# Layer 0 of a two-layer graph-attention kernel: per-node sums in sixteen 32x32 tiles of TensorE in place of four 64x64 tiles

## The chip, the cores and the metric

The kernel runs on one core of a Trainium2 chip. The metric is device time in microseconds (us), from the start to the end of one execution; lower is better. The core has five engines with a queue of instructions each: TensorE (PE; its weight loads are shown apart as PEld), VectorE (DVE), ScalarE (ACT), GpSimd (POOL) and SyncE (SP). Sixteen DMA engines move data between the chip's memory and the on-chip memory (128 partitions). [...]

## The reference

Eight graphs share one adjacency of 2048 nodes, and each node has 256 float32 features. Two attention layers are applied, each with a residual and a layer norm over the features:

```python
# layer 0
e = leaky_relu(einsum('bnd,bmd->bnm', x @ W1, x @ W2), 0.2)
e = where(adj > 0, e, -1e12)
x = layernorm(x + relu(einsum('bnm,bmd->bnd', softmax(e), x @ W3)))
# layer 1: 4 heads of 64; q = x @ W
e = leaky_relu(e_src[:, :, None, :] + e_dst[:, None, :, :], 0.2)
e = where(adj > 0, e, -9e15)
x = layernorm(x + elu(einsum('bijh,bjhd->bihd', softmax(e, axis=2), q)))
```

The adjacency is sparse (each entry is set with a chance of 1/256, then made symmetric, and each node is its own neighbour), so a node has about 17 neighbours, and only their rows are needed.

## The kernel before

**Nodes, tiles, units.** Nodes are ranked by their number of neighbours and cut into 16 tiles of 128 nodes. Tile `t` has `SLOTS[t]` slots (36, 23, 22, 20, 20, 19, 18, 17, 17, 16, 16, 15, 14, 14, 13, 11): slot `k` of a tile is the k-th neighbour of each of its 128 nodes. The eight graphs are worked in two halves `h` of `HB` = 4 graphs. A *unit* is one tile, one half and one layer; there are 32 units for each layer. In layer 0 units with 16 slots or more are cut in two *parts* (22 of the 32 units), the others have one. Tile 0 has 26 main slots and one extra row that serves its ten rare further slots, so a half has 281 main slots, and layer 0 has 562.

**A slot of layer 0.** POOL issues an indirect DMA (`gather`, L203) that brings 128 rows of 4 x 256 float32 (512 KB) into half of a ring tile. There are 16 ring tiles of two slots (`RING`, `CHUNK`) and three more that are held for other use. DVE makes the four dot products of each row with the node's own projected row (`dots`, L726). After the last slot of a part come the softmax steps (`logits0`, `weights0`). ACT then writes, for each slot and each of the four graphs `b`, a 128x64 matrix `dg` with the node's weight on two stacked 64x64 diagonals (`weighted`, L936: `twice` scaled by one column of weights). PE adds weight times row into the accumulators as a matmul of that diagonal with the gathered rows (`add_slot`, L900): eight matmuls of a 64x64 tile, each over 256 columns, for two halves `r` of the nodes, two pairs `c` of graphs, and two graphs `j` in a pair. Each float32 matmul shows as two records in the trace, so a slot has 16. The four (r, c) tiles of the array are independent. The sum of a part lies in two accumulators, `acc[r]`, with partition 64c + node-of-half and column j*256 + feature; `psa` has four banks, so the two of the next part are free while one part is being read. When PE is done with a ring tile, the tile is free for a later gather (`credits`).

**Joining and finishing.** At slot 4 of a second part ACT copies the accumulators of the first part into `hs` (L1023), scaled by the share `u.fs` that the first part keeps in the joint softmax (`spread_shares`, L875); DVE adds the second part's (L1037). In a unit of one part ACT copies (L1041). PE transposes `hs` (`turn`, L501), multiplies by W3 (`project`, L509), DVE applies relu and adds the residual `u.xr` (`residual`, L1054), and the layer norm, the store to `x1s`, the projection for layer 1 (`queries`, L1095), its own terms (`own_terms`, L1111) and the scatter to the table `qg` (`store`, L211) follow. All of these carry the order (half, pair): partition 64c + p holds node p of half r in columns r*512. So `before0` first gathers the node's own rows in node order into one buffer `xo` (`own_rows`), and four SP DMAs (L703) rearrange it into `u.xr`; the x1 rows in `x1s` are kept in that order too, and layer 1 reads them back with one DMA (L1290). The scatter to `qg` goes in two DMAs with half rows.

**The order of work.** Python generators write the instructions of DVE, ACT and PE in a fixed order, the calendar: `tick` runs once for each slot that PE sums; in it `due(n, ...)` events fall n ticks later, ACT draws diagonals two slots ahead (`AHEAD`), and DVE runs up to the next part's slots plus 9 ahead (`SLACK`). Each engine works strictly in its written order and waits on semaphores.

**Layer 1** (L1290 and later) gathers rows of `qg`, DVE or ACT scales them by the weights, and PE sums them with `ident` in four 64x64 tiles. It shares `add_slot` with layer 0.

Of the kernel before, what the change touches and what calls it, by code (L numbers as in the profile page):

```python
# [27 lines left out]
H = 4  # L28
# [111 lines left out]
def fast_path(  # L140
# [43 lines left out]
    dp = ctx.enter_context(tc.tile_pool(name="diag", bufs=4))  # L184
# [46 lines left out]
    q_rows = held[2][:, 2 * KC * C :][:, : 2 * (QW + 2 * H)].rearrange("p (r w) -> p r w", r=2)  # L231
# [8 lines left out]
    twice = const.tile([P, 64], F32, tag="twice", name="twice")  # L240
    nc.vector.tensor_tensor(twice, ident[:, :64], ident[:, 64:], ALU.add)
# [33 lines left out]
    spare = q_rows.rearrange("p r w -> p (r w)")  # L275
# [255 lines left out]
    class Unit:  # L531
        def __init__(self, layer, h, t):
# [22 lines left out]
            self.xo = None  # L555
            self.ready = self.turned = False
# [135 lines left out]
    def own_rows(u):  # L692
        u.xo = xo_rows
        gather(u.xo, xg[u.h][:, :], order[:, u.t : u.t + 1])

    def before0(u):
        while u.xo is None:
            yield
        xo = u.xo
        u.xr = xrp.tile([P, 2, HW], F32, tag="xr", name=f"xr_{u.name}")  # L700
        for r in range(2):
            for c in range(2):
                nc.sync.dma_start(  # L703
                    u.xr[64 * c : 64 * c + 64, r, :], xo[64 * r : 64 * r + 64, ts(c, HW)]
                )
# [3 lines left out]
        turn(xo, f"x_{u.name}", xT)  # L709
        u.turned = True  # L710
# [120 lines left out]
    def weights0(u, i, K, e, m):  # L831
# [7 lines left out]
        if i == len(u.parts) - 1:  # L839
# [5 lines left out]
            if i:  # L845
                due(2, spread_shares, u, e[:, :, 0])
# [19 lines left out]

    def spread_shares(u, f):

        G = 2 if u.layer == 0 else HG // 2
        fs = sp.tile([P, 2, G], F32, tag=f"f{u.layer}", name=f"f_{u.name}", bufs=2 - u.layer)  # L870
# [15 lines left out]
    def add_slot(acc, k, K, rows, diag):  # L886

        for j in range(1 if diag is None else 2):  # L890
            for c in range(2):
                for r in range(2):
                    rr = slice(64 * r, 64 * r + 64)
                    if diag is None:
                        out, lhsT = acc[r][64 * c : 64 * c + 64, :], ident[rr, rr]
                        rhs = rows[rr, ts(c, 2 * CD)].rearrange("p (j w) -> p j w", j=2)[:, :, :C]
                    else:
                        out, lhsT = acc[r][64 * c : 64 * c + 64, ts(j, C)], diag[rr, 2 * c + j, :]
                        rhs = rows[rr, ts(2 * c + j, C)]
# [130 lines left out]
    def after0(u):  # L1030
# [57 lines left out]
        def queries(r):  # L1088
            if r == 0:
                u.qrow = q_rows  # L1090
# [694 lines left out]
```

## Time and profile before

| what | value |
|---|---|
| median of 12 runs | 2449.03 us (2440.92 to 2455.49) |
| the profiled execution's own time | 2447.55 us |
| span of its profile | 2445.6 us |
| matmuls of layer 0's sums (L900, `acc<-s,dg`) | 8992 records, 152.9 to 1422.0 us of the span |
| matmuls of layer 1's sums (L900, `acc<-s,ident`) | 4496 records, 1424.2 to 2426.2 us |
| diagonals (L936) | 2248 of 128x64, mean 340 ns |
| dot products (L726) | 2248 of 128x256, mean 419 ns |
| first part's copies to `hs` (L1023) | 88 of 128x256, mean 463 ns |
| second part's additions on DVE (L1037) | 44 of 128x512, mean 680 ns |
| rearranging DMAs `xr<-held` (L703) | 128 of 128 KB |
| DMA in all | 734.64 MB, mean 300 GB/s |

The 2445.6 us thus fall into a setup of some 153 us, 1270 us of layer 0, and 1020 us of layer 1. The engines run at the same time, so the busy times are not a sum. Durations in a row are those of one instruction from start to end; instructions of one engine overlap at their ends, so the pitch of a series (first start to last end, divided by its number) is smaller than the mean duration.

### The profile page before, as it was taken

The numbers are of one execution on the slowest core, as the hardware profiler recorded it, in microseconds if no ns is written. First come the engines' busy times: TensorE is split into PE (matmuls) and PEld (weight loads), VectorE is DVE, ScalarE is ACT, GpSimd is POOL, SyncE is SP. The second block draws the span as 40 slices with busy tenths as digits, with TensorE's granted clock in tenths as the row PEclk, the third lists the DMA queues.
The fourth block names the chain that finished last, engine by engine and source line by source line (L and its number), as shares of the span: only waits on it lengthen the run. The fifth ranks groups of instructions, "written<-read, shape, count | busy, mean of one in ns | idle before, by whom it ended". The sixth has DMA issues, their size and how long they took to land. (4 is left out here: it accounts for less than half of the span.)

```text
span 2445.6 us, 50606 instructions
## 1 busy us (share of the span) xinstructions
PE 2039.0 (83%) x16234; PEld 1086.2 (44%) x16234; DVE 1950.1 (80%) x6799; ACT 1405.2 (57%) x4803; POOL 1438.0 (59%) x1411
## 2 busy tenths in 40 slices
PE   5158999889889999999999988888788788888885
PEld 2135565556555566656666532222233222332331
DVE  7398788888978886888788568788877787887877
ACT  6035676566666677777677565443554646443545
POOL 3254555555655656555555566667666666766662
PEclk9578898999999999999999998888888887888888
DMA  9987999888887889898888799988998998989981
GB/s 379 340 286 260 303 312 321 264 310 276 294 288 239 292 297 305 302 303 284 304 280 299 261 339 333 322 312 313 331 338 310 316 347 306 337 307 331 329 305 42
DMA packets 239648, 734.64 MB, mean 300 GB/s; under 512 B 53456, under 2 KB 62800, under 8 KB 236944
## 3 DMA queue, kind: packets, MB, share of 16 engines
q0 software_dynamic: 182784, 645.78, 75.6%
q1 hardware_dynamic: 55360, 84.44, 10.2%
q8 instruction: 132, 2.16, 0.3%
q14 instruction: 140, 1.15, 0.1%
q10 hardware_dynamic: 1232, 1.11, 0.1%
HBM read 674.46 MB, written 76.02 MB: 307 GB/s over the span
## 5 line engine op out<-in xcount | busy, mean ns | idle before, releaser
L900 PE MATMUL acc<-s,ident 64*64 64x512 f32 x4496 | 808.6, 681 | 166.3 <-issue 134.4
L203 POOL DMA_INDIRECT s<-xg,idx x564 | 593.5, 1052 | 498.9 <-PE acc L900 268.1
L726 DVE CUSTOM_DVE_ANT_0 j<-s,held 128x256 bf16<-128x256 f32 x2248 | 798.6, 419 | 65.3 <-DMA s<-xg,idx 51.4
L900 PE MATMUL acc<-s,dg 64*64 64x256 f32 x8992 | 707.5, 399 | 103.5 <-issue 56.7
L203 POOL DMA_INDIRECT s<-qg,idx x564 | 569.0, 1009 | 293.3 <-issue 144.7
L936 ACT ACTIVATE dg<-twice,e 128x64 f32<-128x64 f32 x2248 | 574.6, 340 | 88.3 <-remote 46.5
L900 PEld LDWEIGHTS acc<-s,ident 64*64 64x64 f32 x4496 | 284.6, 150 | 678.3 <-issue 608.9
L900 PEld LDWEIGHTS acc<-s,dg 64*64 64x64 f32 x8992 | 390.5, 137 | 374.7 <-issue 199.8
L983 DVE TENSOR_TENSOR s<-s,p 128x2048 f32<-128x2048 f32 (+1 forms) x246 | 542.3, 2208 | 0.1
L973 ACT ACTIVATE s<-s,e 128x64 f32<-128x64 f32 x1376 | 343.5, 335 | 73.1 <-DVE e L1238 32.2
L726 DVE DVE_READ_ACCUMULATOR2_ANT e<- 128x1 f32 x2248 | 180.8, 80 | 0.5 <-DMA s<-xg,idx 0.3
L211 POOL DMA_INDIRECT out_dram<-o,oidx x128 | 128.6, 1005 | 72.2 <-ACT o L487 34.8
L1434 ACT ACTIVATE e<-e 128x40 f32<-128x40 f32 (+19 forms) x88 | 27.4, 312 | 219.8 <-issue 93.2
L1095 PE MATMUL ps_q<-wqs,x1T 128*128 128x264 f32 x512 | 134.1, 402 | 6.7 <-issue 2.9
L509 PE MATMUL ps_p_g<-held,xT 128*128 128x256 f32 x512 | 126.4, 400 | 15.6 <-ACT xT L1434 14.0
L509 PE MATMUL ps_p_h<-held,hT 128*128 128x256 f32 x512 | 121.8, 390 | 0.1
L509 PEld LDWEIGHTS ps_p_g<-held,xT 128*128 128x128 f32 x512 | 99.3, 199 | 42.1 <-ACT xT L1434 14.6
L1095 PEld LDWEIGHTS ps_q<-wqs,x1T 128*128 128x128 f32 x512 | 93.7, 192 | 46.6 <-issue 22.9
L1434 ACT COPY held<-ps_q 128x264 f32<-128x264 f32 x128 | 46.4, 379 | 115.3 <-PE ps_q L1095 87.3
L509 PEld LDWEIGHTS ps_p_h<-held,hT 128*128 128x128 f32 x512 | 95.9, 193 | 27.0 <-issue 13.6
L1054 DVE SCALAR_TENSOR_TENSOR y<-ps_p_h,xr 128x512 f32<-128x512 f32 x64 | 44.0, 687 | 79.0 <-PE ps_p_h L509 52.9
L1162 DVE TENSOR_TENSOR e<-s,own 128x32 f32<-128x32 f32 (+1 forms) x290 | 52.3, 184 | 63.3 <-DMA s<-qg,idx 57.0
(206 smaller groups left out, 1554.4 us busy)
## 6 DMA issues: line engine op xcount, KB each, us to landing
adj<-in_adj_dram SPq DMA_DIRECT2D x16, 1024.0 KB
xr<-held SPq DMA_DIRECT2D x128, 128.0 KB
x1s<-y SPq DMA_DIRECT2D x32, 512.0 KB
xr<-x1s SPq DMA_DIRECT2D x32, 512.0 KB
s<-xg,idx POOLq DMA_INDIRECT x564
s<-qg,idx POOLq DMA_INDIRECT x564
edges<-adj SPq DMA_DIRECT2D x16, 512.0 KB
xg<-in_x_dram SPq DMA_DIRECT2D x4, 2048.0 KB
```

The costliest lines, as they stand in the source:

```text
L203: nc.gpsimd.indirect_dma_start(out=dst, out_offset=None, in_=table, in_offset=AT(ap=index, axis=0), bounds_check=table.shape[0] - 1, oob_i ...
L211: ins = nc.gpsimd.indirect_dma_start(out=table, out_offset=AT(ap=index, axis=0), in_=src, in_offset=None)
L509: nc.tensor.matmul(pp[:, ts(j, C)], lhsT=srcT[:, ts((2 * i + j) * KC + k, P)], rhs=weight[:, k, :], start=(k == 0), stop=(k == KC - 1),)
L726: nc.vector.tensor_tensor_reduce(out=jt, in0=rows[:, ts(b, C)], in1=others(b), scale=1.0, scalar=0.0, op0=ALU.mult, op1=ALU.add, accum_out ...
L900: nc.tensor.matmul(out, lhsT=lhsT, rhs=rhs, start=(k == 0 and j == 0), stop=(k == K - 1 and (j == 1 or diag is None)), tile_position=(64 * ...
L936: nc.scalar.activation(diag[:, b, :], twice, AF.Copy, scale=u.p[i][:, b, k : k + 1])
L973: nc.scalar.activation(v[:, a, g, :], v[:, a, g, :], AF.Copy, scale=pv[:, a, g : g + 1])
L983: nc.vector.tensor_tensor(v, v, pv.unsqueeze(3).to_broadcast([P, n, H, D]), ALU.mult)
L1054: nc.vector.scalar_tensor_tensor(u.y[:, ts(i, 512)], pp, 0.0, u.xr[:, i, :], ALU.max, ALU.add)
L1095: nc.tensor.matmul(pq[:, : C + 2 * H], lhsT=u.x1T[:, ts(i * KC + k, P)], rhs=w.sqs[:, k, j * H : j * H + CD + H], start=(k == 0), stop=(k ...
L1162: nc.vector.tensor_tensor(e[:, k : k + ns, :].rearrange("p s (b g) -> p s b g", b=HB), rows[:, :ns, :].rearrange("p s (b w) -> p s b w", b ...
L1434: heappop(events)[2]()
```

## The change

Layer 0's slots go into a new function, `add_slot0`, with 16 matmuls of a 32x32 tile, one for each quarter `r` of the nodes and each graph `b`, and so 32 records. The diagonals are 128x32 (`four` in place of `twice`), and `diag` has eight buffers in place of four. A part's sum lies in four accumulators `acc[r]`, of which 256 columns are used; these are all four banks of `psa`. At the end of each part ACT copies the four to `hs`: those of a first part scaled by its share (which `sums0` waits for), those of a last part plainly. Before a second part is copied, PE adds the first part's `hs` to the accumulators with `ident` (4 matmuls, 8 records). The transposes read `hs` in the new order, and the copy to `hT` puts the nodes back in order, so that the residual can be the gathered row itself: `own_rows` gathers straight into `u.xr` (one time in five into the old buffer), and the four rearranging DMAs are gone. x1, the queries and the scatter are in node order as well: one scatter in place of two, three DMAs of own terms in place of four, six query copies in place of four. Layer 1 keeps its order and therefore reads x1 with four DMAs in place of one. The transposes of `hs` come one tick after the last part, the projection five (before: six and ten for a split unit).

```diff
-    dp = ctx.enter_context(tc.tile_pool(name="diag", bufs=4))
+    dp = ctx.enter_context(tc.tile_pool(name="diag", bufs=8))
...
     def own_rows(u):
-        u.xo = xo_rows
-        gather(u.xo, xg[u.h][:, :], order[:, u.t : u.t + 1])
+        if u.index % 5 == 3:
+            u.xr = xo_rows
+        else:
+            u.xr = xrp.tile([P, HC], F32, tag="xr", name=f"xr_{u.name}")
+        gather(u.xr, xg[u.h][:, :], order[:, u.t : u.t + 1])
...
-        u.xr = xrp.tile([P, 2, HW], F32, tag="xr", name=f"xr_{u.name}")
-        for r in range(2):
-            for c in range(2):
-                nc.sync.dma_start(
-                    u.xr[64 * c : 64 * c + 64, r, :], xo[64 * r : 64 * r + 64, ts(c, HW)]
-                )
...
+    def add_slot0(acc, rows, diag, first, last):
+
+        for b in range(HB):
+            for r in range(4):
+                rr = slice(32 * r, 32 * r + 32)
+                nc.tensor.matmul(
+                    acc[r][32 * b : 32 * b + 32, :C],
+                    lhsT=diag[rr, b, :],
+                    rhs=rows[rr, ts(b, C)],
+                    start=first,
+                    stop=last,
+                    tile_position=(32 * r, 32 * b),
+                )
...
-                    diag = dp.tile([P, HB, 64], F32, tag="dg", name=f"dg_{u.name}_{i}_{k}")
+                    diag = dp.tile([P, HB, 32], F32, tag="dg", name=f"dg_{u.name}_{i}_{k}")
                     for b in range(HB):
                         nc.scalar.activation(
-                            diag[:, b, :], twice, AF.Copy, scale=u.p[i][:, b, k : k + 1]
+                            diag[:, b, :], four, AF.Copy, scale=u.p[i][:, b, k : k + 1]
                         )
...
                 if acc is None:
-                    acc = [acc_tile(f"acc_{u.name}_{i}_{r}") for r in range(2)]
+                    acc = [acc_tile(f"acc_{u.name}_{i}_{r}") for r in range(4)]
...
-                if i == 1 and k == 4:
-                    u.hs = hs_rows
-                    for r in range(2):
-                        for j in range(2):
-                            nc.scalar.activation(
-                                u.hs[:, ts(2 * r + j, C)], u.accs[0][r][:, ts(j, C)], AF.Copy,
-                                scale=u.fs[:, r, j : j + 1],
+                if k == part.K - 1:
+                    last = i == len(u.parts) - 1
+                    for r in range(4 * i):
+                        nc.tensor.matmul(
+                            acc[r][:, :C], lhsT=ident, rhs=u.hs[:, ts(r, C)], start=False, stop=True
+                        )
+                    while not last and u.fs is None:
+                        yield 0
+                    for r in range(4):
+                        v = u.hs[:, ts(r, C)]
+                        if last:
+                            due(0, nc.scalar.copy, v, acc[r][:, :C])
+                        else:
+                            due(
+                                0, partial(nc.scalar.activation, scale=u.fs[:, r : r + 1]),
+                                v, acc[r][:, :C], AF.Copy,
                             )
                 yield 1
...
-        def whole():
-            if len(u.parts) == 2:
-                for r in range(2):
-                    v = u.hs[:, ts(r, HW)]
-                    nc.vector.tensor_tensor(v, v, u.accs[1][r], ALU.add)
...
+            by_node = u.hT[:, :HC].rearrange("p (b k r n) -> p k r b n", b=HB, k=KC, r=4)
+            for k in range(KC):
+                pt = ps_tile(f"ps_t_h_{n}_{k}")
+                for r in range(4):
+                    nc.tensor.transpose(
+                        pt[:, ts(r, P)], u.hs[:, r * C + k * P : r * C + k * P + P], ident
+                    )
+                due(2, nc.scalar.copy, by_node[:, k], pt.rearrange("p (r b n) -> p r b n", r=4, b=HB))
...
-            for r in range(2):
-                scatter(
-                    f"q{h}",
-                    qg[h].rearrange("n (q c) -> (n q) c", q=2),
-                    orderP[:, t, r : r + 1],
-                    u.qrow[:, r, H : H + QW],
-                )
+            scatter(f"q{h}", qg[h][:, :], order[:, t : t + 1], u.qrow[:, H : H + HB * CD])
...
-        at = 4 if split else 2
-        due(at, whole)
-        due(at + 2, turn_h)
-        due(at + 6, project_h)
+        due(1, turn_h)
+        due(5, project_h)
...
     def sums1(u):
-        nc.sync.dma_start(u.xr.rearrange("p r c -> p (r c)"), x1s[u.h][ts(u.t, P), :])
+        for r in range(2):
+            for c in range(2):
+                nc.sync.dma_start(
+                    u.xr[64 * c : 64 * c + 64, r, :],
+                    x1s[u.h][u.t * P + 64 * r : u.t * P + 64 * r + 64, ts(c, HW)],
+                )
...
-        free = m < 5 or m - 5 in rested and clock[0] >= rested[m - 5] + 4
-        if m < min(opened[0] + 4, 2 * NT) and free and (m == 0 or units[m - 1].turned):
+        free = m < 4 or m == 4 and listed[up[2]]
+        free = free or m - 5 in rested and clock[0] >= rested[m - 5] + 4
+        if m < min(opened[0] + 4, 2 * NT) and free:
```

## The prediction

> **What bounds the kernel now.** I read the busy time by stage first. Columns: stretch in us, its length, then busy us (instructions) of PE, PEld, DVE, ACT and POOL, the granted PE clock, the busy share of the DMA engines, GB/s.
>
> ```profile
> 152.00:1424.00 1272.00, 1159.21 (x11406) 758.52 (x11406) 1033.66 (x5412) 851.66 (x3025) 706.64 (x676) 0.95 0.86 290
> 1424.00:2440.00 1016.00, 828.95 (x4604) 298.65 (x4600) 818.09 (x1118) 504.23 (x1716) 674.16 (x669) 0.85 0.86 308
> ```
>
> The first row is layer 0, the stage that the change rewrites: 1272 us for 32 units, 39.7 us each. PE is busy 91% of it, the DMA engines 86%, DVE 81%, ACT 67%. The change hardly touches the second row.
>
> Then PE's timeline over a unit (start, length, instruction, count of records, idle before it):
>
> ```profile
> 1160.30 4.88 PE L509 MATMUL ps_p_g<-held,xT 128*128 128x256 f32 x16
> 1165.11 3.68 PE L900 MATMUL acc<-s,dg 64*64 64x256 f32 x64
> 1168.73 1.09 PE L501 MATMUL ps_t_x<-ident,y 128*128 128x128 f32 x8
> 1169.75 1.17 PE L900 MATMUL acc<-s,dg 64*64 64x256 f32 x16
> ...
> 1179.42 3.72 PE L509 MATMUL ps_p_h<-held,hT 128*128 128x256 f32 x16
> 1183.08 1.09 PE L900 MATMUL acc<-s,dg 64*64 64x256 f32 x16
> 1184.10 2.05 PE L1095 MATMUL ps_q<-wqs,x1T 128*128 128x264 f32 x8
> 1186.08 2.82 PE L900 MATMUL acc<-s,dg 64*64 64x256 f32 x48
> 1188.83 1.09 PE L501 MATMUL ps_t_x<-ident,held 128*128 128x128 f32 x8
> ...
> 1199.76 4.01 PE L509 MATMUL ps_p_g<-held,xT 128*128 128x256 f32 x16
> ```
>
> From one `ps_p_g` to the next are 39.5 us. From 1160.3 to 1190 PE goes from one block to the next with almost no gap; after that it waits for diagonals. So PE sets the pace for some 30 of 39.5 us, 0.75 of a unit. Two prices come from the starts: a block of 64 records (four slots) takes 1168.73-1165.11 = 3.62 us and one of 16 takes 1184.10-1183.08 = 1.02 us, so a slot costs (3.62-1.02)/3 = 0.867 us and the change to other work 0.15 us. A 128-wide record costs 3.72/16 = 0.23 us.
>
> ACT's timeline over the same stretch:
>
> ```profile
> 1163.99 0.58 ACT L717 COPY held<-ps_p_g 128x512 f32<-128x512 f32 x1 [2.48 <-PE ps_p_g L509]
> 1185.29 0.38 ACT L1434 COPY held<-ps_q 128x264 f32<-128x264 f32 x1 [4.37 <-PE ps_q L1095]
> 1187.42 1.55 ACT L1023 ACTIVATE held<-acc,f 128x256 f32<-128x256 f32 x4
> 1192.32 2.98 ACT L936 ACTIVATE dg<-twice,e 128x64 f32<-128x64 f32 x12
> ```
>
> ACT stands 2.48 and 4.37 us until PE is done: here PE is late, not ACT. A slot's four diagonals cost ACT 4 x 2.98/12 = 0.99 us, four copies from the accumulators 1.55 us. Last the waits, over the whole span (total, times, longest):
>
> ```profile
> POOL s L203 <- PE acc L900: 300.2, 167, 10.6
> ACT held L1434 <- PE ps_q L1095: 87.3, 66, 5.0
> DVE y L1054 <- PE ps_p_h L509: 52.9, 20, 5.4
> DVE j L726 <- DMA s<-xg,idx: 51.4, 23, 27.1
> ```
>
> Gathers stand until PE frees a ring tile, ACT until PE has the queries, DVE until PE has projected; DVE waits for rows far less. A PE that falls behind starves DMA and DVE, which then catch up at their own limit.
>
> **Slots on PE.** A slot goes from 16 records over four tiles (four rounds of 0.867/4 = 0.217 us) to 32 records of the same 256 columns over sixteen tiles. If sixteen run side by side, that is two rounds, 0.434 us; it can't be less, since each tile has two passes. If only four run at once, as now, it is eight rounds, 1.73 us. No row shows a 32x32 tile. I take 0.434 us: the nearest row is L900 itself, whose tiles already run independently. In windows of 40 ns four weight loads begin (columns as above):
>
> ```profile
> 1004.15:1004.19 0.04, 0.04 (x8) 0.02 (x4) 0.03 (x1) 0.04 (x1) 0.00 (x0) 1.00 1.17 256
> 1004.37:1004.41 0.04, 0.04 (x8) 0.03 (x4) 0.01 (x1) 0.04 (x1) 0.00 (x0) 1.00 1.45 359
> ```
>
> At that spacing (at most 10 ns) sixteen begin within 160 ns, inside a round. 562 slots x (0.867-0.434) = **-243 us of PE**.
>
> [...]
>
> **The join.** 22 split units x 8 records x 0.23 = **+41 us of PE**. It replaces 44 additions on DVE of 0.68 us: -30 us of DVE, 22 small products (0.16 us, the 128x4 rows) come back: **-26 us of DVE**.
>
> **The end of a part: a new wait.** Four accumulators are all that there is, so the next part's first slot waits until ACT has copied all four. Behind it in PE's queue stand `ps_p_g`, transposes and projections, and ACT and DVE wait for those. For a part without a join, 22 first parts and 10 whole units: 1.55 us of copies and, for two semaphores and the drain of the last matmul, some 0.45 us (three times the 0.15 us above): 2.0 us. For the 22 joined parts most copies run beside the later joins, and 0.9 us is left. 32 x 2.0 + 22 x 0.9 = **+84 us of PE**. Lower end 0 (PE has caught up and would wait for diagonals anyway); upper end: ACT comes to the copies behind two slots' diagonals, 2 x 0.99 us more at each of 54 ends, +191 us in all. I take the middle row, because ACT's order writes the copies right after the diagonals of the last slot or of one more.
>
> **ACT.** 32 columns less: from the copies of 264 (379 ns) and 512 columns (586 ns), 0.83 ns a column, 27 ns x 2248 = -60 us. Added: the last parts' copies, 22 x 1.55 + 10 x (1.55-1.16) = +38 us, and two 4-column query copies a unit, 64 x 0.16 = +10 us. Some -12 us on an engine that is 67% busy and waits for PE: 0 on the path. The copy to `hT` in another order I price like now (0.586 us); at double it would be 64 x 0.59 = 37 us of ACT, hidden while ACT waits for PE.
>
> **DMA and queues.** The 128 rearranging DMAs (16.8 MB of some 369 MB in layer 0, so about 50 us of the engines' 1094) go, and SP issues four DMAs a unit less. The own rows no longer pass through one buffer that four DMAs and eight transposes must leave first. POOL issues one scatter a unit less (32 x 1.07 = 34 us of 707). DMA isn't last here as long as PE is, so 0 on the path; with all of it on the path it would be -50. Layer 1 reads x1 in pieces of 2048 bytes: in the trace's packet records those took 113 ns, those of 4096 bytes 179 ns in layer 1, so 4096 x (2 x 113 - 179) ns / 16 = **+12 us** of DMA in a stage whose DMA is 86% busy on average and over 90% in most slices. I count all of it; 0 if the early reads hide it.
>
> **The sum.** PE: -243 + 41 + 84 = -118 us, of which 0.75 lies where PE sets the pace: -88. DVE's -26 us counts for the other quarter: -6. Layer 1 +12. Together -82 us: the profiled execution's 2447.55 becomes 2365.5, and the median, 1.5 us above it, **2367 us**. What is late next is DVE: it would be 1008 of some 1180 us busy, 85%. The floor below which PE doesn't help is the DMA, (1094-50)/0.96, if it kept up 0.96, 1088 us: 1272-1088 = 184 us at most, 2449-184+12 = 2277.
>
> **Rivals.**
> (1) *PE's time was hidden, and DVE and DMA are the bound.* For it: in half of the 20-us stretches DVE is over 90% busy and DMA at 0.9 or more. Against it: the gathers' 300 us of waiting is for PE. Then only the DVE term (all 26) and layer 1's 12 remain: 2435 us, between 2425 and 2455. Chance 0.14.
> (2) *The round trip at part ends decides (slower).* Place: the first slot after each of the 54 part ends in PE's queue. It decides from (243-41)/54 = 3.7 us each, where nothing is left. With 5.5 us (ACT's copies behind diagonals, and query copies that themselves wait for PE): (297-202) x 0.75 + 12 = +83, 2532 us. For it: ACT waits up to 5.0 us for `ps_q`, and the copies queue behind such work. Against it: while PE waits, ACT draws ahead, and PE, now twice as fast as ACT on a slot (0.43 against 0.99 - 4 x 0.027 = 0.88 us), catches up. Chance 0.16.
> (3) *The tiles don't run sixteen abreast.* Eight abreast or a bound on issue: slots at 0.87, +125 x 0.75 + 12 = 2555 us. Four abreast: 562 x 0.867 = +487 us more, all on the path, 3100 us or so. For it: no row here has such tiles, and 64 loads and matmuls a slot are twice as many as now. Chance 0.11.
>
> **How the numbers follow.** The forecast (2277 to 2425) has 0.59. The runs before spread over 0.6%, so 0.2%, 5 us, is about what a measurement tells from no change. Rival 1 gives 0.09 to faster, 0.04 to the same, 0.01 to slower; the others are slower. Faster 0.68, same 0.04, slower 0.28. The range goes from 2285, a little inside the DMA's floor, to 2500, which cuts off rival 3 and half of rival 2, 0.19 in all. The likeliest case's own range is 2285 to 2425.
>
> **What would show it.** Right: layer 0's sums end near 1340 instead of 1422; blocks of 32 records grow by some 0.43 us a slot; the gathers' wait for PE shrinks. The part ends: PE idle of about 2 us before the first slot, released by the copies. Wrong: blocks of 0.87 us or more a slot (rival 3); PE waits of 4 us and more for the copies (rival 2); shorter slots with gathers no longer waiting, and the same end (rival 1). Layer 1 should be 12 us longer at most; if it differs by more, something that I left out lies there.

## The result, and the profile after

The changed kernel takes 2551.12 us (median of 11 runs, 2541.27 to 2564.24) where the kernel before takes 2449.11: a ratio of 1.0414, 95% interval 1.0399 to 1.0428. It is slower by 102 us; the prediction had it faster by 82.

Where the time went shows by stage. The windows of the changed kernel, with the columns of the rows before (stretch, length, busy us and instructions of PE, PEld, DVE, ACT and POOL, granted PE clock, DMA share, GB/s):

```profile
149.00:1530.00 1381.00, 1257.44 (x20622) 740.93 (x20622) 1017.28 (x5397) 822.85 (x3192) 671.10 (x648) 0.92 0.77 257
1530.00:2548.00 1018.00, 825.02 (x4586) 294.56 (x4584) 813.74 (x1108) 503.30 (x1713) 675.38 (x664) 0.83 0.88 306
```

Layer 0 has grown from 1272 to 1381 us; layer 1 is as long as it was. PE has 20,622 matmul records in layer 0 where it had 11,406, is busy 98 us longer, and still holds 91% of the stage. DVE, ACT and POOL are a little less busy than before, and the DMA engines fall from 0.86 to 0.77: all others wait more. The waits of the changed kernel (total us, times, longest) say for whom:

```profile
POOL s L203 <- PE acc L915: 475.5, 230, 7.3
...
DVE y L1094 <- PE ps_p_h L512: 98.8, 21, 14.4
...
ACT held L1471 <- PE acc L915: 90.0, 27, 9.2
ACT held L1471 <- PE acc L1057: 86.6, 29, 5.5
```

The gathers' wait for PE went from 300 to 476 us and DVE's wait for `ps_p_h` from 53 to 99 us. ACT now stands in front of the copies at part ends until PE has finished the sums; the prediction had PE standing for ACT. So PE is late, and what makes it late has no releaser. PE's timeline over a stretch of a unit (start, length, instruction, records, idle time before it with its releaser):

```profile
1165.95 0.73 PE L915 MATMUL acc<-s,dg 32*32 32x256 f32 x32
1166.61 2.05 PE L1133 MATMUL ps_q<-wqs,x1T 128*128 128x264 f32 x8
1168.59 0.71 PE L915 MATMUL acc<-s,dg 32*32 32x256 f32 x32
1170.03 4.58 PE L915 MATMUL acc<-s,dg 32*32 32x256 f32 x115 [0.72 <-ACT held L1471]
1174.92 1.37 PE L915 MATMUL acc<-s,dg 32*32 32x256 f32 x7 [0.31 <-issue]
1176.44 0.59 PE L915 MATMUL acc<-s,dg 32*32 32x256 f32 x2 [0.16 <-issue]
1177.21 0.38 PE L915 MATMUL acc<-s,dg 32*32 32x256 f32 x1 [0.18 <-issue]
1177.92 2.15 PE L915 MATMUL acc<-s,dg 32*32 32x256 f32 x54 [0.33 <-issue]
```

A slot by itself (32 records, 415 ns each on average) takes 0.71 to 0.73 us, less than the 1.09 of before (16 records of 399 ns): the small tiles do run side by side. But from 1174.9 to 1177.9 us PE executes ten matmul records, a few at a time, some 0.75 us apart. It waits for no semaphore there ("issue" is idle time in which nothing that the profile shows was waited for). I call a *halt* a distance of 0.46 us or more between the starts of two neighbouring records of PE or PEld in layer 0 of which neither names a wait. The kernel before had 170 halts, 111.9 us in all; the changed one has 318, 189.1 us.

The kernel before had them in the very unit that the prediction reads, between the lines that it shows:

```profile
1196.05 0.37 PE L900 MATMUL acc<-s,dg 64*64 64x256 f32 x1 [0.28 <-issue]
1196.78 0.45 PE L900 MATMUL acc<-s,dg 64*64 64x256 f32 x2 [0.35 <-issue]
1197.54 1.25 PE L900 MATMUL acc<-s,dg 64*64 64x256 f32 x10 [0.32 <-issue]
1199.07 0.76 PE L900 MATMUL acc<-s,dg 64*64 64x256 f32 x7 [0.28 <-issue]
```

Something besides the records has grown as well. One of the two queues that carry instructions, from the list of DMA queues (packets, MB, share of 16 engines), first before, then after:

```profile
q8 instruction: 132, 2.16, 0.3%
```

```profile
q8 instruction: 203, 3.33, 0.5%
```

Each packet is 16,384 bytes in the trace. PE and PEld have 33,394 records before and 51,718 after (waits for semaphores among them), 253 and 255 for each packet. The other such queue, q14, has 140 packets before and 139 after. From these counts I infer that q8 brings PE's instructions, in blocks of some 256.

### The profile page after: what moved, and what is told of

Read it like the earlier page. It is cut to its first block, busy times and chain, and to the rows that moved or that the text cites. A ratio compares the mean times of both kernels' runs of the same rounds, so it can differ in the third digit from the quotient of the medians.

```text
span 2548.1 us, 68746 instructions
## 1 busy us (share of the span) xinstructions
PE 2131.0 (84%) x25434; PEld 1063.5 (42%) x25434; DVE 1930.5 (76%) x6779; ACT 1375.7 (54%) x4969; POOL 1401.7 (55%) x1379
## 4 chain that ended last, share of the span: by engine, by line
PE 61%; issue 12%; DVE 9%; DMA 7%; ACT 5%; POOL 3%; another core or an unknown queue 2%; SPq 1%; POOLq 0%; ACTq 0%; DVEq 0%
PE acc L915 26%; PE acc L929 15%; PE ps_q L1133 5%; PE ps_p_h L512 4%; PE ps_p_g L512 4%; DVE s L1020 4%; PE ps_t_x L504 3%; POOL s L203 2%; DMA s<-qg,idx 2%; PE acc L1057 2%; DMA s<-xg,idx 2%; DVE j L724 1%; PE ps_t_h L1082 1%; ACT s L1010 1%
## 5 line engine op out<-in xcount | busy, mean ns | idle before, releaser
L203 POOL DMA_INDIRECT s<-xg,idx x564 | 586.8, 1041 | 670.0 <-PE acc L915 457.1
L915 PE MATMUL acc<-s,dg 32*32 32x256 f32 x17984 | 751.9, 415 | 140.6 <-issue 58.6
L203 POOL DMA_INDIRECT s<-qg,idx x564 | 573.8, 1017 | 299.0 <-issue 145.6
L915 PEld LDWEIGHTS acc<-s,dg 32*32 32x32 f32 x17984 | 329.9, 107 | 500.9 <-issue 335.4
L973 ACT ACTIVATE dg<-four,e 128x32 f32<-128x32 f32 x2248 | 512.2, 317 | 6.0 <-DVE e L840 6.0
L1094 DVE SCALAR_TENSOR_TENSOR y<-ps_p_h,xr 128x512 f32<-128x512 f32 x52 | 35.7, 687 | 116.6 <-PE ps_p_h L512 94.2
L1471 ACT COPY held<-acc 128x256 f32<-128x256 f32 x128 | 42.4, 380 | 146.6 <-PE acc L1057 86.6
L1471 ACT COPY held<-ps_q 128x4 f32<-128x4 f32 (+1 forms) x192 | 49.2, 311 | 119.0 <-PE ps_q L1133 105.3
```

The lines of the kernel that those rows point to most:

```text
L203: nc.gpsimd.indirect_dma_start(out=dst, out_offset=None, in_=table, in_offset=AT(ap=index, axis=0), bounds_check=table.shape[0] - 1, oob_i ...
L915: nc.tensor.matmul(acc[r][32 * b : 32 * b + 32, :C], lhsT=diag[rr, b, :], rhs=rows[rr, ts(b, C)], start=first, stop=last, tile_position=(3 ...
L973: nc.scalar.activation(diag[:, b, :], four, AF.Copy, scale=u.p[i][:, b, k : k + 1])
L1471: heappop(events)[2]()
```

## The experiments

**Two kinds of chip.** The kernel before ran in six jobs: the first comparison, whose chip has no number on record, and five on chips of different numbers. It took 2449.11 us in the first comparison, 2450.55 on chip 15 (e9 to e12) and 2448.21 on chip 6 (e13 to e15), but 2195.92 on chip 14 (e1 to e4), 2196.69 on chip 13 (e5 to e8) and 2198.23 on chip 7 (e16, e17). I call the chips of the first three jobs kind A and those of the other three kind B; the names stand for these two groups of times and for nothing else. Ratios are therefore always against the kernel before in the same job, and layer 0 is compared within a kind. This is the kernel before on A, from the list of groups (busy us, mean ns of one, idle before, releaser):

```profile
L726 DVE CUSTOM_DVE_ANT_0 j<-s,held 128x256 bf16<-128x256 f32 x2248 | 798.6, 419 | 65.3 <-DMA s<-xg,idx 51.4
L900 PE MATMUL acc<-s,dg 64*64 64x256 f32 x8992 | 707.5, 399 | 103.5 <-issue 56.7
```

and on B (run e6, below):

```profile
L726 DVE CUSTOM_DVE_ANT_0 j<-s,held 128x256 bf16<-128x256 f32 x2248 | 797.7, 418 | 64.5 <-DMA s<-xg,idx 53.8
...
L900 PE MATMUL acc<-s,dg 64*64 64x256 f32 x8992 | 595.9, 393 | 70.8 <-ACT dg L936 70.5
```

A dot product or a matmul lasts as long on B, but the same matmuls keep PE busy 112 us less, and what ends PE's idle time is ACT, no longer "issue". On B the kernel before has no halt at all.

The results that stand beside each other, in one table (e2, e8, e13 and e16 follow in the text). Records are those of PE and PEld in layer 0, waits for semaphores among them; layer 0 and halts are in us; a pair of labels is the same kernel on A and on B:

| kernel | records | A: layer 0 | halts | ratio | B: layer 0 | halts | ratio |
|---|---|---|---|---|---|---|---|
| before (and e6) | 23,392 | 1271 | 112 | 1 | 1120 | 0 | 1 |
| new order alone (e11, e1) | 23,408 | 1226 | 82 | 0.9807 | 1107 | 0 | 0.9926 |
| + copies and join (e14, e3) | 23,711 | 1237 | 48 | 0.9832 | 1144 | 1 | 1.0085 |
| changed (first, e5) | 41,751 | 1382 | 189 | 1.0414 | 1121 | 40 | 0.9912 |
| changed again (e10) | 41,751 | 1379 | 187 | 1.0395 | | | |
| before, split matmuls (e12, e4) | 41,376 | 1425 | 260 | 1.0652 | 1145 | 32 | 1.0098 |
| changed, split matmuls (e9, e17) | 77,719 | 1769 | 360 | 1.2007 | 1582 | 275 | 1.202 |
| no first part end (e15, e7) | 41,439 | 1377 | 194 | 1.0434 | 1110 | 27 | 0.9925 |

### The change taken apart: e1, e2, e3

The changed kernel with 64x64 tiles again, 16 records a slot, diagonals of 64 columns, two accumulators and the join on DVE; the new order of nodes and the gathering of own rows stay (e1). Then with the copies at every part end and the join on PE (e2), then with four accumulators of 256 columns, so that no part has a second set (e3).

```diff
-                    add_slot0(acc, rows[:, s, :], diag, k == 0, i == 0 and k == part.K - 1)
+                    add_slot(acc, k, part.K, rows[:, s, :], diag)
...
-                    acc = [acc_tile(f"acc_{u.name}_{i}_{r}") for r in range(4)]
+                    acc = [acc_tile(f"acc_{u.name}_{i}_{r}") for r in range(2)]
```

> The change without its 32x32 tiles: node order, own rows gathered in place, one scatter, four x1 loads in layer 1 as changed; slots of four 64x64 tiles, 64-column diagonals, two accumulators, joining by DVE at slot 4 as before. Theory CODE (the 32x32 slots double PE's instructions, 64 a slot with the weight loads in place of 32, and PE halts where its instruction stream is not there yet): 2410 to 2450 us, as before or a little faster, since 16.8 MB of DMA and 32 scatters are gone. Theory TRIP (ACT and PE wait for each other at each part end, since the next part needs the same four accumulators): also 2410 to 2450. Theory ORDER (the node order itself costs, by the strided copy to hT, more query copies, four x1 loads): 2500 or more.

> e1 with the copies at each part's end and the join on PE, as changed, but two accumulators of 512 columns, so that two more are free for the next part. CODE: e1 plus the join's 41 us on PE and some waiting, 2440 to 2480. TRIP: ACT still stands in its queue until PE ends a part, but PE goes on; 2460 to 2500, and the step from here to e3 is the larger one. ORDER: like e1, 2500 or more.

> e2 with the sums in four accumulators of 256 columns, so that each next part waits for ACT's copies, as changed; still 64x64 tiles and half of the changed kernel's PE instructions for the slots. It differs from the changed kernel in the tile size of the slots alone. TRIP: at least as slow as the changed kernel, 2540 to 2620, since its slots need 0.87 us of array time in place of 0.43. CODE: faster than the changed kernel, 2460 to 2510, with the standing at PE without a semaphore back at some 110 us from 190.

The chip was of kind B, while the expectations are in times of kind A, so the ratios are what can be compared: e1 0.9926 (0.991 to 0.9943), e2 1.0102 (1.0083 to 1.0121), e3 1.0085 (1.0068 to 1.0102). The order of nodes is a gain of 16 us. The copies and the join cost some 40 us there (e1 to e2). One set of accumulators in place of two costs nothing (e2 to e3), so with 64x64 tiles on B PE does not suffer from waiting for the copies.

### More instructions and nothing else: e4

The kernel before, with each 256-column matmul of a slot cut into two of 128: the same tiles, columns and sums, but 64 loads and matmuls a slot instead of 32, as many as the changed kernel has.

```diff
-        for j in range(1 if diag is None else 2):
+        for i in range(1 if diag is None else 4):
+            j, s = divmod(i, 2)
...
-                        out, lhsT = acc[r][64 * c : 64 * c + 64, ts(j, C)], diag[rr, 2 * c + j, :]
-                        rhs = rows[rr, ts(2 * c + j, C)]
+                        out = acc[r][64 * c : 64 * c + 64, ts(i, C // 2)]
+                        lhsT = diag[rr, 2 * c + j, :]
+                        rhs = rows[rr, ts(2 * (2 * c + j) + s, C // 2)]
...
```

> The kernel before, each matmul of layer 0's slots cut in two of 128 columns: the same sums and columns, 32 records a slot with 32 weight loads, as many instructions as the 32x32 slots. CODE: slower by 60 to 150 us, 2510 to 2600, with the standing without a semaphore near 190 us. TRIP and ORDER: 2449 within 15 us, apart from what a slot's block gains in length in the timeline (0.87 us now), which is to be read beside it.

On B 1.0098 (1.0082 to 1.0115), 24 us, and 24 halts (32 us) appear where there was none. That is less than CODE had expected (60 to 150 us) and more than the other theories (15 us at most). Since all these runs stood at 2196 us for the kernel before, the changed kernel itself had to be run on such a chip.

### The same kernels on the other kind of chip, and the round trip: e5 to e8

e5 is the changed kernel, e6 the kernel before, both as they are. e7 leaves out what happens at the end of a first part: the scaling by its share, the four copies and the join. e8 lets ACT draw diagonals four slots ahead (`AHEAD = 4`).

```diff
-                    for r in range(4 * i):
-                        nc.tensor.matmul(
-                            acc[r][:, :C], lhsT=ident, rhs=u.hs[:, ts(r, C)], start=False, stop=True
-                        )
-                    while not last and u.fs is None:
-                        yield 0
-                    for r in range(4):
+                    for r in range(4 if last else 0):
...
```

> The changed kernel itself, on one chip with the next ones, to stand beside e1 to e4. The chip of e1 to e4 ran the kernel before in 2196 us, with next to none of PE's standing without a semaphore. TRIP: there the changed kernel is near e3 (1.0085 of before), 1.00 to 1.02. CODE: standing doubles with the instructions wherever there is any; on a chip with none of it in the kernel before 1.00 to 1.03, on a chip with 111 us of it in the kernel before again 1.03 to 1.05.

> The kernel before, for its profile on this chip: the standing of PE without a semaphore in layer 0 beside e5's. CODE: the difference of the two, 0.75 to 1 of it, is most of e5's loss on a chip where there is standing; TRIP: the loss stays where there is none.

> The changed kernel with both parts of a unit summed in one accumulation: the scaling of the first part by its share, its copies to hs and the join on PE are left out (22 part ends of 54, 88 copies, 176 join records). TRIP: ACT stands some 4 us less at 22 ends and the join's 41 us goes, so 0.75 x (88 + 41), 80 to 120 us faster than e5. CODE: only the join and the copies count, 20 to 50 us faster than e5.

> The changed kernel with ACT drawing diagonals four slots ahead in place of two (AHEAD 4; the eight diagonal buffers of the change hold them). TRIP: at a part's end PE has four slots ready when the copies are done, and ACT's standing before them is covered by its lead; 30 to 100 us faster than e5. CODE: within 20 us of e5.

On B the changed kernel is a little *faster*: 0.9912 (0.9885 to 0.994), below what either theory had expected (1.00 at least). e7 is at 0.9925 (0.9906 to 0.9945) and e8 at 0.9921 (0.9893 to 0.9948), no different; for e7 both theories had expected a gain (20 us at least), for e8 TRIP alone (30 us at least). The sign of the change depends on the chip, and neither the part ends nor the diagonals' lead decide it there. In e5 the slots' matmuls stand in the groups with

```profile
L915 PE MATMUL acc<-s,dg 32*32 32x256 f32 x17984 | 506.4, 397 | 120.9 <-ACT dg L973 80.9
```

where e6 had 595.9: on B PE does save on the slots, 90 us. The kernel also has its first halts on B, 30 of 0.5 to 3.7 us. Counted in records of PE and PEld from the start of the program, some of them stand at

```
11457  12737  12993  14273  17089  17345  17601  19137
```

whose distances (1280, 256, 1280, 2816, 256, 256, 1536) are all multiples of 256, the block of the instruction queue. Of the 30 halts, 27 stand at this place in a block, 37.6 of 39.6 us. That speaks for the theory called CODE since e1, that TensorE is not *fed* fast enough: what counts is the number of its instructions, not their work.

### Dose, again on kind A: e9 to e12

e9 cuts each slot matmul of the changed kernel in two, as e4 did with the kernel before. In its expectation "64 matmuls" are the 64 loads and matmuls of a slot, which become 128. The other three repeat the changed kernel, e1's and e4's.

```diff
-        for b in range(HB):
+        for i in range(2 * HB):
+            b, s = divmod(i, 2)
...
-                    acc[r][32 * b : 32 * b + 32, :C],
+                    acc[r][32 * b : 32 * b + 32, ts(s, C // 2)],
                     lhsT=diag[rr, b, :],
-                    rhs=rows[rr, ts(b, C)],
+                    rhs=rows[rr, ts(2 * b + s, C // 2)],
...
```

> The changed kernel with each slot's 64 matmuls cut into two of 128 columns, so 128 pairs of load and matmul a slot; the same columns, sums and results. By the theory that TensorE must be fed its instructions (CODE) the price grows with the count: cutting the kernel before from 32 to 64 a slot cost 1.0% on a chip where the changed kernel stood at 0.991, and this adds twice as many instructions (about 34,000 records), with more halts without a wait and at multiples of 256 records: 1.02 to 1.06 there, and on a chip where the changed kernel stands at 1.04, 1.08 to 1.25. By the theory of the round trip at part ends (ROUND TRIP) it is within 0.5% of the changed kernel in the same job.

> The changed kernel as it is, for the others of this job. If this chip is like the one of e5 to e8, 0.991; if it is like the chip of the first comparison, 1.041. By CODE the halts without a wait in layer 0 come to about 40 us in the first case and 190 us in the second; by ROUND TRIP the ratio is above 1.03 on every chip.

> The change without 32x32 tiles, copies at part ends and joining on TensorE (as e1): as many instructions a slot as before. By CODE the chip decides little: 0.990 to 1.002 on either kind. By a theory that the new order of rows and their gathering costs the time (ORDER), it is above 1.03 wherever the changed kernel is.

> The kernel before with its slot matmuls cut in two (as e4): as many instructions a slot as the changed kernel, none of the rest. By CODE 1.01 on a chip where the changed kernel is at 0.99, and 1.03 to 1.08 where it is at 1.04; by ROUND TRIP and by ORDER it is at 1.01 on either.

The chip was of kind A. e9 1.2007 (1.1975 to 1.204), e10 1.0395 (1.0367 to 1.0423), e11 0.9807 (0.9779 to 0.9835), e12 1.0652 (1.0621 to 1.0683). The kernel before with nothing but its matmuls cut in two loses 6.5%, more than the whole change loses. Its groups:

```profile
L902 PE MATMUL acc<-s,dg 64*64 64x128 f32 x17984 | 794.3, 289 | 195.3 <-issue 161.5
...
L902 PEld LDWEIGHTS acc<-s,dg 64*64 64x64 f32 x17984 | 611.1, 141 | 378.4 <-issue 309.9
```

One matmul has become shorter (399 to 289 ns) with half the columns, but PE's idle time by "issue" has gone from 56.7 to 161.5 us. Layer 0 grew by 154 us, the halts by 148. So the number of PE's instructions is enough for such a loss; the round trip and the order of nodes are not needed for it. e11 came out below what CODE had expected (0.990 to 1.002): the order alone is worth more on A, with 82 us of halts for 112; why it has fewer wasn't tried. In e9 the halts come to 360 us:

```profile
L916 PE MATMUL acc<-s,dg 32*32 32x128 f32 x35968 | 996.6, 299 | 269.3 <-issue 211.2
...
L916 PEld LDWEIGHTS acc<-s,dg 32*32 32x32 f32 x35968 | 704.6, 111 | 551.3 <-issue 443.2
```

**The halts of A are of another sort than those of B.** On B they stand at one place in the blocks of 256. On A they stand anywhere: 4 of the changed kernel's 318 (2.9 of 189 us) are at that place, none of the 170 before, 1 of e12's 420, and 50 of e9's 538 (70 of 360 us), where the expectation had them at multiples of 256. What they go with is POOL. Of the 318, 311 begin within 1.5 us after the start of one of POOL's indirect DMAs (which take about 1.05 us each), while only 44% of the records lie there. Before it is 170 of 170 halts (69% of the records), in e12 414 of 420 (51%), in e9 513 of 538 (26%); in e5 on B it is 25 of 30 (75%). That the gathers cause these halts is not shown, since no run takes them away from the real sums.

### The feed by itself, and the rest on kind A: e13 to e15

e13 leaves the whole computation out. PE alone runs matmuls of 32x32 tiles straight on, in four stretches: 32 and 256 columns with no DMA, then the same two beside loads. Each of the 4,096 matmuls of a stretch shows as two pairs of records, so a stretch has 16,384 records. The weights, and the rows without DMA, are zeros, and no DMA is an indirect one.

```python
def pairs(width, rhs):
    for i in range(PAIRS // 16):
        for b in range(4):
            for r in range(4):
                rr = slice(32 * r, 32 * r + 32)
                nc.tensor.matmul(acc[r][32 * b : 32 * b + 32, :width], lhsT=diag[rr, ts(b % 2, 32)],
                    rhs=rhs[rr, :width], start=True, stop=True, tile_position=(32 * r, 32 * b))
...
```

e14 is e3's kernel, e15 is e7's.

> Not the kernel: it leaves out the whole computation and writes zeros. TensorE alone runs four stretches of 4,096 pairs of load and matmul in 32x32 tiles, straight on: with 32 columns and with 256 columns while no DMA runs, then the same two while 60 loads of 2 MB keep the DMA engines busy. What it measures is how fast TensorE is fed. CODE expects the 32-column stretches, whose array time is an eighth of the other's, to be bound by feeding: at the 16 KB packets of the instruction queue (256 instructions each, about 0.8 us from start to end) one at a time 4,096 pairs take 26 us or more, and more under traffic, with halts at multiples of 128 or 256 instructions; on a chip of the first kind longer than on the other by over 20%. A theory that the halts are a clock or array matter, not a matter of feeding (ARRAY), expects no halts in the 32-column stretches and no difference under traffic.

> As e3: the new order, copies and joining on TensorE, four sums, but 64x64 tiles, so half the changed kernel's instructions a slot. If the chip is of the first kind (before near 2449): CODE expects 0.995 to 1.010, some 35 to 45 us above the kernel of e11 and 75 us or more below the changed kernel; ROUND TRIP expects 1.03 or more. On the other kind 1.008, as before.

> As e7: the changed kernel leaves out the scaling of the first part by its share, its copies and the joining, so its output differs. On a chip of the first kind ROUND TRIP expects at least 60 of the 100 us lost to come back (ratio 1.015 or less); CODE expects 0 to 45 us back (1.020 to 1.040), since the 64 instructions of a slot stay. On the other kind 0.992, as before.

The chip was of kind A again. PE's timeline in e13 with 32 columns, no DMA:

```profile
100.45 1.53 PE L81 MATMUL acc<-rows,diag 32*32 32x32 f32 x128 [2.20 <-issue]
103.91 1.53 PE L81 MATMUL acc<-rows,diag 32*32 32x32 f32 x128 [1.92 <-issue]
107.36 1.53 PE L81 MATMUL acc<-rows,diag 32*32 32x32 f32 x128 [1.93 <-issue]
...
602.10 1.53 PE L81 MATMUL acc<-first,diag 32*32 32x32 f32 x128 [4.69 <-issue]
608.32 1.53 PE L81 MATMUL acc<-first,diag 32*32 32x32 f32 x128 [4.69 <-issue]
```

128 matmul records and as many loads run in 1.53 us, then PE stands for 2 us, and so on through the stretch; the last two lines are the stretch beside the loads, where it stands for 4.7. The steps are of 256 records exactly, and there is no semaphore in this stream. Each halt ends 1.2 to 1.6 us after a packet of the instruction queue has ended, all 253 of them; so do the 27 and 134 halts at this place in e5 and e17 on B (1.0 to 1.7 us). Over whole stretches a block of 256 takes 3.56 us with 32 columns and 3.66 with 256, though the second's matmuls have eight times the columns. Beside 410 GB/s of loads it takes 6.25. A stretch of 32 columns in quiet took 228 us, not the 26 us or more that CODE had put down by packets of about 0.8 us: in the profiles of the kernel before and the changed one a packet of this queue took 1.03 us on average and 0.88 at least, and most of a block's 3.56 us lies outside it. So in e13 PE got 256/3.6 = 71 instructions a microsecond in quiet and 41 beside that traffic: 14 to 24 ns each. For these halts the theory that they belong to the array (ARRAY) falls. The other sort, that of the kernels on A, doesn't occur here, though the chip is of kind A. (The last stretch, of 256 columns, ran after the loads had ended and says 3.70.)

e14 is at 0.9832 (0.981 to 0.9855) and e15 at 1.0434 (1.0407 to 1.0461). Leaving the first part's end out brings nothing back (CODE had expected 0 to 45 us), so the round trip is out on A too; the copies and the join cost little there (2407.4 us against e11's 2401.0), less than the 35 to 45 us that CODE had expected. What remains between e14 and the changed kernel is the 32x32 tiles with their doubled instructions, and what goes with them (diagonals of 32 columns with more buffers, the shares for four quarters). The groups of e14, whose row in the changed kernel is 751.9 us:

```profile
L899 PE MATMUL acc<-s,dg 64*64 64x256 f32 x8992 | 658.5, 395 | 97.0 <-ACT dg L936 33.2
```

```profile
L915 PE MATMUL acc<-s,dg 32*32 32x256 f32 x17984 | 751.9, 415 | 140.6 <-issue 58.6
```

Layer 0 is 145 us longer with the small tiles, and the halts are 141 us more.

### Clock or traffic, and the other kind of chip: e16, e17

e16 is e13 with the two stretches beside the loads in the other order and twice the loads; it too leaves the computation out. e17 is e9's kernel.

> As e13, with the two stretches beside DMA traffic in the other order and 120 loads: 256 columns first. It leaves out the whole computation. In e13 a block of 256 instructions took 3.6 us without traffic, with 32 and with 256 columns alike, and 6.2 us beside traffic, where the granted clock had also fallen to 0.5. FEED (the limit is the fetch of the next 16 KB block) expects the 256-column stretch beside traffic at 5.5 to 6.5 us a block, whatever the clock; a theory that the low clock made the second rate (CLOCK) expects 3.6 to 4 us as long as the granted clock stays above 0.8. If the chip is of the other kind, FEED expects fewer or shorter halts: under 2.8 us a block without traffic.

> As e9. If the chip is of the first kind (before near 2449), 1.20 again; if it is of the other, CODE expects 1.01 to 1.06 with halts at multiples of 256 records, ROUND TRIP 0.99.

The chip was of kind B. The windows of e16 (here without ACT, which ran nothing) for 32 columns in quiet, 256 and 32 columns beside loads, and 32 columns after the loads:

```profile
28.00:227.00 199.00, 83.64 (x6993) 76.93 (x6995) 0.00 (x0) 0.00 (x0) 1.00 0.02 4
...
522.00:862.00 340.00, 214.18 (x6984) 143.63 (x6958) 0.00 (x0) 0.37 (x1) 0.70 1.02 409
911.00:1152.00 241.00, 59.62 (x4995) 54.36 (x4985) 0.00 (x0) 0.00 (x0) 0.50 0.97 381
1155.00:1225.00 70.00, 29.31 (x2462) 26.74 (x2465) 0.00 (x0) 0.00 (x0) 0.50 0.02 4
```

Dividing each stretch by its records, a block takes 3.64, 6.24, 6.18 and 3.64 us. The granted clock fell to 0.70 in the second stretch, so the condition written for it (above 0.8) wasn't met; the last line decides in its place: at a clock of 0.50 without loads PE was fed as fast as at 1.00. The slower feed belongs to the traffic. And the feed is the same on both kinds of chip (3.56 us a block in quiet and 6.25 beside loads on A, 3.64 and 6.18 to 6.24 on B), where a difference of over 20% had been expected.

e17 is at 1.202 (1.1981 to 1.2059), where CODE had expected 1.01 to 1.06 on B. By e13's numbers such a loss was to be expected: 77,719 records are 304 blocks, which at e13's rates would take an estimated 304 x 3.6 = 1094 to 304 x 6.2 = 1885 us. Layer 0 took 1582 us here and 1769 on A. On B 134 of its 135 halts stand at the block's place, 274 us of the 461 by which layer 0 is longer than in e5; so there the feed holds PE up. On A most of e9's halts are of the other sort.

**A version that beats both on A.** The new order with the old tiles (e11) takes 2401 us there, 0.9807 of the kernel before. On B it (e1) is at 0.9926 and the changed kernel at 0.9912, within each other's intervals.

## Why the prediction was wrong, step by step

**Slots on PE, the step that failed.** "It can't be less, since each tile has two passes" stands as a floor: no slot was shorter (0.64 us the shortest, below). But the floor of 0.434 us, from the time of the array alone, was taken as the price. That 64 loads and matmuls must reach PE was mentioned under rival 3 and has no price in the sum. Two things were missing.

First, in long blocks a slot costs more than the floor: on B, where halts are few, the shortest blocks of one to four slots take 0.64, 1.42, 2.05 and 2.69 us, so (2.69-0.64)/3 = 0.68 us for a further slot. That alone makes the term 562 x (0.867-0.68) = -105 us in place of -243.

Second, twice the instructions bring halts. On A, e12 shows it with nothing else changed: +154 us of layer 0, 148 us of it halts; from e14 to the changed kernel it is +145 us, with 141 us more of halts. The prediction's -182 us on the path (243 x 0.75) became +145 there. On B the change leaves a gain, 23 us from e3 to e5, with 39 us of halts in it. Those are halts of the feed: by e13 and e16 an estimated 0.9 us for 64 instructions in quiet and 1.56 beside the heaviest traffic, where the 32 of before would take 0.45 to 0.78 and stay under the 0.867 us that their slot took. On A nearly all the halts are of the other sort, which these rates don't explain.

**"After that it waits for diagonals."** The idle time after 1190 us in the unit that the prediction reads was in part something else. Three of the starts shown in the result section, 1196.05, 1197.5 and 1199.07, end halts of 0.65 to 0.71 us, and none of these names a diagonal. The sign that PE was short of something other than work stood in that stretch.

**Sixteen starts within 160 ns.** Held in the first slot of a block: in the shortest slots of the changed kernel's trace both sets of sixteen records start 6.7 ns apart, with 0.14 us between them. In the slots that follow in a block most starts are 16 to 17 ns apart. The loss came by another way.

**The blocks of 256.** The prediction did not price them. In the changed kernel on B most blocks end without a halt: 27 of e5's halts stand at a block's end, and PE has some 160 blocks in layer 0 (41,751 records). In a stream without pauses none does: in e13 PE stands 2 us at every block in quiet and 4.7 us beside traffic.

**The join and the ends of parts.** The join's records keep PE busy 51.5 us (predicted 41). PE's time from its last record of a part to its next slot is on average 1.6 us at the 32 ends without a join and some 1.8 us at the joined ones, about 90 us (predicted 84). As a count of PE's time that was near. As a price on the path it wasn't: without the first part's end nothing comes back on A (e15) or B (e7). Copies and join together cost 6 us on A (e11 to e14, two jobs) and 35 to 41 on B (e1 to e3 and e2).

**ACT, 0 on the path.** Held, with a turn: ACT idles 219 us in front of the copies at part ends on A and 76 on B, nearly all of it ended by PE. It is late after PE, not before it.

**DMA and queues, the order of nodes.** Priced at 0, "with all of it on the path it would be -50". The new order of nodes with its fewer DMAs is worth 16 us on B and 50 us on A (e1, e11; on A PE also halts 30 us less): the one part of the change that pays on both, and it was under-priced.

**Layer 1, +12 us.** What follows layer 0's sums took 1021.5 us before and 1017.4 after. The smaller reads are hidden, the lower end that the text had named.

**The rivals.** Rival 3 named "a bound on issue" with 2555 us, and 2551 was measured. That the two numbers are so near is luck: the price went by 0.87 us a slot (eight tiles abreast or a slow issue), and that is not how it happens. A slot alone is shorter, and the halts lie between; on B the same kernel gains. Rival 2 gave 2532 by PE waits of 5.5 us at part ends; they are 1.7. Rival 1's hidden PE time is excluded by the gathers, which wait for PE longer than before; what was said for it, DVE over 90% busy and DMA at 0.9 or more in half of the 20-us stretches, holds for both at once in 13 of the 63. Of the signs listed, "layer 0's sums end near 1340" shows the failure plainly: they end at 1526.0.

**What stays open.** Why PE halts on A while POOL issues gathers, and on B hardly. In such a halt PE got three to eight records every 0.73 us or so. These halts are there in the kernel before too, and grow with the number of instructions (table); whether the loads or the matmuls count wasn't separated. Bare streams are fed alike on both kinds (3.56 and 3.64 us a block in quiet), DVE's and ACT's instructions last alike (in layer 0 of the changed kernel DVE was busy 1017 us and ACT 823 on A, 1009 and 819 on B, with the same numbers of instructions within 0.2%), and 4096-byte packets took 190 ns on A and 182 on B. What makes A different wasn't found. A run that keeps the sums on real data and leaves the gathers out would test POOL's part.

## What to carry to other kernels

Give the number of instructions a price of its own beside the time of the array. In the streams without pauses (e13, e16) PE got 256 of them in 3.6 us in quiet and 6.2 beside 410 GB/s, 14 to 24 ns each; as an estimate from these runs, take the larger of the two prices where PE runs on over more than a block. That is not the whole price: on A the step from 32 to 64 instructions a slot cost 154 us over 562 slots (e12), 0.27 us a slot, by halts that these rates don't give. So test it, which costs little: cut every matmul of the kernel before in two and change nothing else; the loss shows what doubled instructions cost on that chip. Look for idle PE time under "issue" in the profile before: 57 us of it in the slots' row was the sign that PE already stood at times with no wait that the profile names.

## What the runs showed of the hardware that was not expected

- A stream of matmuls without any wait halted every 256 instructions in e13: 1.53 us of work, 2 us of standing still, 4.7 beside 410 GB/s of loads. It went on 1.2 to 1.6 us after a 16,384-byte packet of the instruction queue had ended. The granted clock made no difference in e16 (0.50 and 1.00: 3.64 us a block each).
- On the chips of kind A, PE had halts of another sort: in the changed kernel 311 of 318 began within 1.5 us of the start of an indirect DMA on POOL, and PE then got a few records every 0.73 us. On kind B they hardly showed: 3 of e5's 30 halts lay away from a block's place.
- The chips differed by more than the change: 2448 to 2451 us on three and 2196 to 2198 on the other three for the same kernel. What differed is PE's pace (busy 707.5 and 595.9 us with the slots' matmuls, 808.6 and 609.8 with those of layer 1), and with the chip the sign of the change (1.0414 and 0.9912).
- In the changed kernel on A, matmuls on 32x32 tiles started 6.7 ns apart in the first slot of a block and mostly 16 to 17 ns apart in those that follow.
